# One product moved behind the next step's cosines, and two table products moved from GpSimd to VectorE, in the second block of a two-block float32 kernel

## The chip, the cores and the metric

The kernel runs on 1 core of a Trainium2 chip. The metric is the device time of one execution in microseconds; for a comparison, the median of several executions. Before the change three executions took 1615.61, 1616.44 and 1616.86 us, so the median is 1616.44 us.

Five engines work on instruction queues of their own and wait for one another through semaphores: TensorE (PE; its weight loads are the row PEld), VectorE (DVE), ScalarE (ACT), GpSimd (POOL) and SyncE (SP), which here issues most of the DMAs. Each engine takes its own instructions in order: an instruction that waits holds up all that stand behind it on that engine.

## The reference, cut to what matters

The program has two blocks. The first (an attention with a conditioning state, then a soft mixture of 64 experts) ends before anything the change touches. The second block works on 2 sequences of 1024 tokens with 256 features and runs two layers of this form, of which the change touches two places, the tables of the rotary embedding and the layer norm ahead of the feed-forward part:

```python
def _layer(x, wqkv, qs, ksc, wo, lg, lb, w1, b1, w2, b2):
    h = shift_token(x)
    q, k, v = jnp.split(h @ wqkv, 3, axis=-1)     # 8 heads of 64
    q = l2norm(q) * qs
    k = l2norm(k) * ksc
    q, k = rotary_xpos(q, k)                      # q*cos*scale + rotate_half(q)*sin*scale; k the same with 1/scale
    o = local_attention(q, k, v)                  # windows of 128 tokens, each with the one before it
    x = x + o @ wo
    h = shift_token(x)
    mu, var = h.mean(-1, keepdims=True), h.var(-1, keepdims=True)
    h = (h - mu) / jnp.sqrt(var + 1e-05) * lg + lb
    a, g = jnp.split(h @ w1 + b1, 2, axis=-1)
    x = x + (a * jax.nn.gelu(g, approximate=False)) @ w2 + b2
```

All is float32.

## The kernel before, in words

**Windows and chunks.** The second block cuts the work of its two layers into 32 windows of 128 tokens for the attention (16 for a layer: 2 sequences of 8) and 8 chunks of 512 tokens for the norm and the feed-forward part (4 for a layer). One Python loop, `for s in range(-2, LAG + 4 * CHUNKS)` with `LAG = 7`, staggers them. In step s the loop projects window s + 2 (`project`, L1121, then `rotate_parts`), computes the scores of window s (`scores`, L1210, and `maxima`, L1227), turns the weights of window s - 1 (`turn_e`, L1271 on PE) and mixes window s - 2 with its values (L1290). At the end of the step `forward(s - LAG)` does a quarter of a chunk: for quarters 0 to 2 two slices of `gate` each (L1371), in quarter 2 also `centre` of the next chunk, in quarter 3 `normalise` of the next chunk and `feed`. For the first chunk no chunk runs ahead of it, so `forward(-2)` in step 5 is `centre(0)` alone, `forward(-1)` in step 6 is `normalise(0)` alone, and `forward(0)` in step 7 begins with `gate(0, 0)`.

**The order.** In this loop the order of PE, VectorE, ScalarE and GpSimd is written out by hand (`manual_schedule` over these four): each runs its instructions in the order of the Python calls. Only the DMA queue of SP is ordered by the framework's planner.

**What `rotate_parts(i)` issues, in order:** ScalarE copies the projected queries and keys `pq` from PSUM to `raw` (L1135) and squares them (L1137). VectorE multiplies `pq` by the cosine tables into `t1` (L1143, "the cosines" below; it starts after L1135). GpSimd multiplies the two swapped halves of `raw` by the sine tables into `t2` (L1145, two instructions, "the sines").

**PSUM buffers.** `two_banks` hands out three buffers in turn. In a step after the sixth they go to `pq`, to the two halves of the scores `sc`, then to `pe` (weights of the window before, first half of the heads), `pt` (L1195) and `pe` again (second half), and then to the gates. So the first `pe` writes where `pq` stood and must wait for L1135 and L1143 to have read it; `pt` writes where the first half of `sc` stood, and the second `pe` where the second half stood, and these wait for the maxima (L1227) on VectorE.

**`normalise(f)`** sums the squares on PE (`pvar`, L1333), makes the inverse root on ScalarE as Ln and Exp (L1353, L1354, each with a table load before it), multiplies `hc` by it on VectorE (L1355, 128x1024) and then scales and shifts `hc` on GpSimd (L1357, two instructions of 128x512). `gate` reads `hc`.

**`divide(i, hg)`** divides the weights of window i by their sums: a reciprocal on VectorE (L1256), then four products of 128x256 (L1260), for the first half of the heads on GpSimd and for the second half on VectorE. It stands at the end of a step: the first half ahead of `forward`, the second behind it.

**`weights2(l, ...)`** loads a layer's weights. For `"tabs"` it loads two tiles of tables by SP (L1019): tile y = 0 holds the cosine tables of q and k, tile y = 1 the sine tables. Each of a tile's two halves is multiplied by the layer's `q_scale` or `k_scale` row (for the sines: rolled by half), 128x512, so four products in all, all on GpSimd (L1021). For the second layer the call stands at the very end of step 13, behind `divide(13, 1)`. The cosines and sines of window 16, the second layer's first, come at the start of step 14.

Of the kernel before, what the change touches and what calls it, by code (L numbers as in the profile page):

```python
# [82 lines left out]
def bcast(ap, axis, n):  # L83

    ap = ap.unsqueeze(axis)
    shape = list(ap.shape)
    shape[axis] = n
    return ap.to_broadcast(shape)
# [3 lines left out]
def tile_kernel(ctx: ExitStack, tc: tile.TileContext, a: dict, out: bass.AP):  # L92
    nc = tc.nc
# [768 lines left out]
    def fetch(i, jj):  # L862
        at = slice(jj * 512, (jj + 1) * 512)
        nc.sync.dma_start(row(i)[:, at], lgd[i][:, at])
# [13 lines left out]
    def scale(i):  # L878
        den = dens.pop(i)
        nc.vector.reciprocal(den, den)  # L880
        nc.vector.tensor_scalar(row(i), row(i), den, None, ALU.mult)
# [84 lines left out]
    y = [mo1.tile([P, NE // 4, D], F32, name="y0"), xp.tile([P, NE // 4, D], F32, tag="y1", name="y1")]  # L966
    dxs = ExitStack()
    dx = dxs.enter_context(tc.tile_pool(name="dx", bufs=2))
    with tc.manual_schedule(
        engines={mybir.EngineType.PE, mybir.EngineType.DVE, mybir.EngineType.Activation}  # L970
    ):
        at_weigh = (1, 3, 4, 6)
        for g in range(2):
            weights(g)
        for it in range(3, ITS):
            n, m = divmod(it, 8)
            if it + 1 < ITS:
                logits(it + 1)
            dispatch(it)
            if n and m in (1, 4):  # L980
                experts(4 * n - 4 + m // 4 * 2)

            i = it - ITS + 8
            if 0 <= i < 4:
                for jj in range(4):
                    fetch(i, jj)
            if i - 1 in at_weigh:
                scale(at_weigh.index(i - 1))
            if i in at_weigh:
                heaviest(at_weigh.index(i))  # L990
                weigh(at_weigh.index(i))
        turn_w(0, 0)
        turn_w(0, 1)
        experts(12)
        combine(0, 0)
        turn_w(0, 2)
        combine(0, 1)
        turn_w(0, 3)
        combine(0, 2)
        experts(14)  # L1000
        dxs.close()
        for t in (xa, xb):
            nc.gpsimd.memset(t[:, :, :, 0:1], 0.0)


        load = {}
        wqo = pphi.tile([P, 4 * D * 4], F32, tag="phi", name="wqo")
        load["wqkv"] = wqo[:, : 6 * INNER].rearrange("p (k n) -> p k n", k=2)
        load["wo"] = wqo[:, 6 * INNER :].rearrange("p (k n) -> p k n", k=4)
        mask = dx0.tile([P, 4 * WIN], F32, tag="l1", name="mask")  # L1010
        nc.sync.dma_start(mask, a["mask"])

        def weights2(l, *names):
            for name in names:
                if name == "tabs":

                    load[name] = [dx0.tile([P, 2, 8, DH], F32, tag="dsp", name=f"tabs{l}{y}") for y in range(2)]
                    for y, t in enumerate(load[name]):
                        nc.sync.dma_start(t, a["tabs"].rearrange("p (x y) w d -> y p x w d", y=2)[y])  # L1019
                        for x, of in enumerate((("qs", "ks"), ("qsr", "ksr"))[y]):  # L1020
                            nc.gpsimd.tensor_tensor(  # L1021
                                t[:, x], t[:, x], bcast(rows[:, ROWS[f"{of}{l}"]], 1, 8), ALU.mult
                            )
                    continue
                k = {"wqkv": 2, "wo": 4, "w1": 2, "w2": NF}[name]
                whole = HID // P if name == "w2" else k
                nc.sync.dma_start(
                    load[name][:, :whole, :], a[name][l, : whole * P].rearrange("(c p) n -> p c n", p=P)
                )
                if whole < k:  # L1030
                    for r0 in (0, TG):
                        nc.sync.dma_start(load[name][r0 : r0 + TAIL, whole, :], a[name][l, whole * P :])

        weights2(0, "wqkv", "tabs", "wo")
# [38 lines left out]
    with tc.manual_schedule(  # L1073
# [10 lines left out]
        ts, nrqs, vs, es, eTs, pos, oTs, hcs, us = {}, {}, {}, {}, {}, {}, {}, {}, {}  # L1084
# [45 lines left out]
        def rotate_parts(i):  # L1130

            w = i % NWIN
            pq = pqs.pop(i)
            raw = dx0.tile([P, 16, DH], F32, tag="keep", name="raw")
            nc.scalar.copy(raw, pq)  # L1135
            sqs[i] = la.tile([P, 16, DH], F32, tag="t", name="sq", bufs=3)
            nc.scalar.activation(sqs[i], raw, AF.Square)  # L1137
            t1 = la.tile([P, 16, DH], F32, tag="t", name="t1", bufs=3)
            t2 = la.tile([P, 16, DH], F32, tag="t2", name="t2", bufs=1)
            hf = DH // 2  # L1140
            p4, r4, t14, t24 = (t.rearrange("p (x h) d -> p x h d", x=2) for t in (pq, raw, t1, t2))
            cos, sin = (t[:, :, w, :] for t in load["tabs"])
            nc.vector.tensor_tensor(t14, p4, bcast(cos, 2, H1), ALU.mult)  # L1143
            for lo, hi in ((0, hf), (hf, DH)):
                nc.gpsimd.tensor_tensor(  # L1145
                    t24[:, :, :, lo:hi], r4[:, :, :, hf - lo : DH - lo], bcast(sin[:, :, lo:hi], 2, H1), ALU.mult
                )
            ts[i] = t1, t2
# [167 lines left out]
        def chunk(f):  # L1316

            return f // (B * 2), f // 2 % B, f % 2 * 512
# [28 lines left out]
        def normalise(f):  # L1347
            l, b, t0 = chunk(f)
            hc, sq = hcs[f], hcs.pop((f, "sq"))
            pv = bank("pvar")  # L1350
            sums(f, pv, [sq[:, k, :] for k in range(2)])
            rs = fa["rs"]
            nc.scalar.activation(rs, pv, AF.Ln, bias=eps5)  # L1353
            nc.scalar.activation(rs, rs, AF.Exp, scale=-0.5)  # L1354
            nc.vector.tensor_tensor(hc, hc, bcast(rs, 1, 2), ALU.mult)  # L1355
            for k in range(2):
                nc.gpsimd.tensor_scalar(  # L1357
                    hc[:, k, :], hc[:, k, :], col(f"lg{l}", k), col(f"lb{l}", k), ALU.mult, ALU.add
                )
# [29 lines left out]
        def feed(f):  # L1389

            l, b, t0 = chunk(f)
            hcs.pop(f)
            py, u = two_banks("py"), us.pop(f)
            for c in range(2):
                for n in range(NW1):
                    nc.tensor.matmul(  # L1396
                        py[:, c, :], load["w2"][:, n, c * P : (c + 1) * P], u[:, n, :], start=(n == 0), stop=False
                    )
            for c in range(2):
                r = slice(c * TG, c * TG + TAIL)  # L1400
                nc.tensor.matmul(
                    py[:, c, :], load["w2"][r, NW1, c * P : (c + 1) * P], u[r, NW1, :], start=False, stop=True
                )
            at = slice(1 + t0, 1 + t0 + 512)
            for c in range(2):
                if l < DEPTH - 1:
                    nc.vector.scalar_tensor_tensor(
                        xa[:, c, b, at], py[:, c, :], col(f"b2{l}", c), xb[:, c, b, at], ALU.add, ALU.add
                    )
                    continue  # L1410
                yo = fa["yo"][:, c, :]
                nc.sync.dma_start(yo, xkeep[f % 4][:, c, :])
                nc.gpsimd.tensor_tensor(yo, yo, xb[:, c, b, at], ALU.add)
                nc.vector.scalar_tensor_tensor(yo, py[:, c, :], col(f"b2{l}", c), yo, ALU.add, ALU.add)
                nc.sync.dma_start(out[c * P : (c + 1) * P, b * S + t0 : b * S + t0 + 512], yo)

        def forward(at):

            f, k = divmod(at, 4)
            if at == -2:  # L1420
                centre(0)
            if at == -1:
                normalise(0)
            if not 0 <= f < CHUNKS:
                return
            if k == 0:
                gate(f, 0)
                gate(f, 1)
            if k == 1:
                gate(f, 2)  # L1430
                gate(f, 3)
            if k == 2:
                gate(f, 4)
                if f + 1 < CHUNKS:
                    centre(f + 1)
                gate(f, 5)
            if k == 3:
                if f + 1 < CHUNKS:
                    normalise(f + 1)
                feed(f)  # L1440


# [29 lines left out]
        LAG = 7  # L1472
        fa = {}
        for s in range(-2, LAG + 4 * CHUNKS):
            now, before, nxt, new = (0 <= s + d < WINDOWS for d in (0, -1, 1, 2))

            if new:
                project(s + 2)
                rotate_parts(s + 2)
            ended = 0 <= s - 2 < WINDOWS  # L1480


# [56 lines left out]
            if s == 5:  # L1539

                f = xp.tile([P, 4 * NS], F32, tag="e", name="f")
# [141 lines left out]
```

## Time and profile before

One execution was profiled. It took 1615.51 us by itself, 0.93 us less than the median of the three; the span from its first to its last instruction is 1613.6 us.

| what | number | where from |
|---|---|---|
| median of the three executions | 1616.44 us | the times |
| the profiled execution's own time | 1615.51 us | the times |
| its span | 1613.6 us | the page |
| mean granted TensorE clock | 0.999 | the clock of the core |
| idle time of PE ahead of L1271, ended by L1143 | 4.0 us in 2 waits, the longest 2.5 | the waits of PE |
| the product with the inverse root, L1355 | 8 times, 1.226 us median | the groups by line |
| idle time of VectorE ahead of L1355 | 28.3 us in 8 waits | the groups by line |
| table products on GpSimd, L1021 | 8 times, 1.274 us median | the groups by line |
| the table DMAs of the second layer, L1019 | issued from 1158.7 us, landed within 5.4 us | the rows on the tables |

A row of a timeline gives the start in us from the span's start, the duration in us, the engine, the line of the kernel, the operation, the tile that is written and those that are read, the shape and the count of instructions that were merged into the row. At the end, in square brackets, stands how long the engine had idled and what released it.

### The profile page before, as it was taken

What the parts mean: (1) busy time and instruction counts of PE and PEld (TensorE: products, weight loads), DVE (VectorE), ACT (ScalarE), POOL (GpSimd) and SP (SyncE); (2) the same over time, 40 slices, a digit from 0 to 9 for tenths busy, and PEclk for the clock granted to TensorE, in tenths of its full rate; (3) what the DMA queues carried; (4) which work ended last, traced back from release to release, by engine and by line L of the source; (5) the groups of instructions that cost most, each with busy time, mean ns of one, the idle gap of its engine ahead of it and who ended that gap; (6) DMA issues with size and microseconds to landing.
All of it is one profiled execution on the core that took longest, in us unless ns stands there. A gap on an engine that the chain in (4) does not pass through costs nothing.

```text
span 1613.6 us, 22646 instructions
## 1 busy us (share of the span) xinstructions
PE 1583.7 (98%) x8660; PEld 803.9 (50%) x8660; DVE 910.0 (56%) x1597; ACT 892.6 (55%) x1662; POOL 539.4 (33%) x830
## 2 busy tenths in 40 slices
PE   8999999999999999999999999999999999999998
PEld 4333333333333444444887666555555555656543
DVE  5768758776773222225355765656575665656532
ACT  2477768777886222226134454666656565666631
POOL 4223323333330100000103345545465555555411
PEclk9999999999999999999999999999999999999999
DMA  5100000010000544555632102000100001000001
GB/s 158 53 14 14 1 15 13 1 21 8 1 1 26 170 137 143 165 168 174 205 124 78 40 1 81 1 1 1 66 1 1 14 1 55 1 8 21 14 13 39
DMA packets 49708, 82.66 MB, mean 51 GB/s; under 512 B 4536, under 2 KB 24928, under 8 KB 49344
## 3 DMA queue, kind: packets, MB, share of 16 engines
q1 hardware_dynamic: 47056, 75.38, 15.2%
q0 software_dynamic: 1584, 5.29, 1.1%
q8 instruction: 68, 1.11, 0.3%
q10 hardware_dynamic: 960, 0.56, 0.1%
q14 instruction: 40, 0.33, 0.1%
HBM read 56.04 MB, written 20.97 MB: 48 GB/s over the span
## 4 chain that ended last, share of the span: by engine, by line
PE 92%; DVE 4%; ACT 1%; issue 1%; DMA 1%; POOL 0%; DVEq 0%; ACTq 0%; POOLq 0%
PE pga L1371 9%; PE sc L329 8%; PE po L347 7%; PE pm L295 7%; PE lg L795 7%; PE sl L821 7%; PE pq L1121 6%; PE cmb L909 5%; PE py L1396 4%; PE pwo L1310 3%; PE sc L1210 3%; PE pe L1271 3%; PE po L1290 3%; PE pv L1177 3%; PE pqk L265 2%; PE py L842 2%
## 5 line engine op out<-in xcount | busy, mean ns | idle before, releaser
L302 DVE TENSOR_REDUCE mx<-pm 128x2 f32<-128x1024 f32 x256 | 302.3, 1219 | 118.2 <-PE pm L295 117.6
L337 ACT ACTIVATE e<-sc 128x512 f32<-128x512 f32 (+1 forms) x500 | 266.1, 611 | 72.2 <-PE pm L295 44.6
L329 PE MATMUL sc<-qs,km 32*128 32x512 f32 x1024 | 254.7, 619 | 0.9 <-DVE qs L317 0.9
L295 PE MATMUL pm<-km,qm 32*128 32x512 f32 x1024 | 246.1, 619 | 2.4 <-ACT xa L432 0.6
L365 POOL TENSOR_TENSOR ob<-ob,part 128x512 f32<-128x512 f32 x101 | 128.3, 1271 | 270.2 <-ACT part L364 270.2
L1260 POOL TENSOR_SCALAR e<-e,den 128x256 f32<-128x256 f32 (+1 forms) x128 | 130.9, 1036 | 31.3 <-DVE den L1256 31.3
L1371 PE MATMUL pga<-hc,w 128*128 128x512 f32 x320 | 141.1, 593 | 0.0
L347 PE MATMUL po<-e,v 128*32 128x512 f32 x1024 | 136.7, 604 | 0.0
L1145 POOL TENSOR_TENSOR t<-raw,tabs 128x512 f32<-128x512 f32 x64 | 81.7, 1299 | 154.7 <-ACT raw L1135 149.4
L329 PEld LDWEIGHTS sc<-qs,km 32*128 32x128 f32 x1024 | 87.6, 183 | 84.6 <-ACT e L337 64.4
L1244 ACT ACTIVATE e<-e,nmx 128x256 f32<-128x256 f32 (+1 forms) x256 | 123.6, 487 | 2.7 <-DVE nmx L1227 2.5
L1121 PE MATMUL pq<-wqo,xa 128*128 128x512 f32 x256 | 115.9, 595 | 1.6 <-DVE xb L897 0.9
L909 PE MATMUL cmb<-xb,y 128*128 128x256 f32 x512 | 116.6, 380 | 0.2 <-ACT xb L895 0.2
L795 PE MATMUL lg<-phi,xa 128*128 128x512 f32 x256 | 115.9, 595 | 0.3 <-ACT xa L432 0.3
L821 PE MATMUL sl<-dsp,xb 128*128 128x512 f32 x256 | 114.9, 592 | 0.0
L295 PEld LDWEIGHTS pm<-km,qm 32*128 32x128 f32 x1024 | 82.9, 183 | 60.0 <-DVE mx L302 31.6
L1227 DVE CUSTOM_DVE_ANT_0 e<-sc,mask,zn 128x256 f32<-128x256 f32 (+1 forms) x256 | 101.9, 460 | 17.3 <-PE sc L1210 17.3
L909 PEld LDWEIGHTS cmb<-xb,y 128*128 128x128 f32 x512 | 94.9, 190 | 16.6 <-issue 3.2
L805 DVE TENSOR_TENSOR l<-lg,keep 128x512 f32<-128x512 f32 x32 | 22.1, 691 | 143.5 <-ACT keep L803 143.5
L1371 PEld LDWEIGHTS pga<-hc,w 128*128 128x128 f32 x320 | 59.2, 190 | 67.2 <-issue 65.1
L1135 ACT COPY raw<-pq 128x1024 f32<-128x1024 f32 x32 | 32.4, 1012 | 107.2 <-PE pq L1121 105.4
L803 ACT COPY keep<-lg 128x512 f32<-128x512 f32 x32 | 18.7, 585 | 125.1 <-issue 107.4
(213 smaller groups left out, 2456.2 us busy)
## 6 DMA issues: line engine op xcount, KB each, us to landing
lgd<-keep SPq DMA_DIRECT2D x64, 256.0 KB, 2.4
w<-in_ffn_W SPq DMA_DIRECT2D x16, 1024.0 KB, 7.0
ebig<-lgd SPq DMA_DIRECT2D x64, 256.0 KB, 3.3
wqo<-in_wqkv SPq DMA_DIRECT2D x2, 1536.0 KB, 7.5
w<-in_w SPq DMA_DIRECT2D x2, 1386.0 KB, 5.9
km<-hk SPq DMA_DIRECT2D x32, 64.0 KB, 2.3
qm<-hq SPq DMA_DIRECT2D x32, 64.0 KB, 2.4
phi<-in_phi SPq DMA_DIRECT2D x1, 2048.0 KB, 7.6
```

Source lines behind the costliest of these rows:

```text
L295: nc.tensor.matmul(pm[:, x, :], qm[u % 2][r, i * P : (i + 1) * P], km[u % 3][r, n * 512 : (n + 1) * 512], start=True, stop=True,)
L302: nc.vector.tensor_reduce(mxs[hu][:, i % 4, 2 * half : 2 * half + 2, n], pm, AX.X, ALU.max)
L329: nc.tensor.matmul(sc[:, x, :] if both else sc[x], km[u % 3][r, j * P : (j + 1) * P], qs[u % 2][r, n * 512 : (n + 1) * 512], start=True, s ...
L337: nc.scalar.activation(part, t, AF.Exp, scale=1.0 / HD0**0.5)
L347: nc.tensor.matmul(po[32 * hh : 32 * hh + 32, :], v[b][:, j, at : at + 32], es[s, hh // 2][:, hh % 2, :], start=True, stop=True,)
L365: nc.gpsimd.tensor_tensor(obs[u, n], obs[u, n], part, ALU.add)
L795: nc.tensor.matmul(lg[:, b, :], xa[:, k, b, 1 + m * P : 1 + (m + 1) * P], phi[:, k, n * 512 : (n + 1) * 512], start=(k == 0), stop=(k == 1),)
L821: nc.tensor.matmul(accs[n][b][:, c, :], xo_tm[:, b * 8 + m, c * P : (c + 1) * P], d[:, b, :], start=(m == 0), stop=(m == 7),)
L909: nc.tensor.matmul(acs[q][:, c, :], y[b][:, 4 * jj + j, c * P : (c + 1) * P], eT[:, j // 2, j % 2 * 256 : (j % 2 + 1) * 256], start=(jj == ...
L1121: nc.tensor.matmul(pq[:, x, :], shifted(xa, k, b, w * WIN, P), load["wqkv"][:, k, x * 512 : (x + 1) * 512], start=(k == 0), stop=(k == 1),)
L1260: engine.tensor_scalar(e[:, x, c, lo:], e[:, x, c, lo:], den[:, x, c : c + 1], None, ALU.mult)
L1371: nc.tensor.matmul(pt[:, x, :], load["w1"][:, k, lo : lo + P], hcs[f][:, k, :], start=(k == 0), stop=(k == 1))
```

## The change

Two edits. First, `normalise` is cut in two: the sums and the inverse root stay, and the products (VectorE's L1355 and GpSimd's two of L1357) go into a new function `normalised`. For every chunk but the first it is called right behind `normalise`, which leaves the order as it was. For the first chunk it is called in step 7, behind `project(9)` and `rotate_parts(9)`: on VectorE the product then stands behind the cosines of window 9 and ahead of the maxima of window 7, on GpSimd the two instructions stand behind the sines of window 9. Second, of the second layer's four table products the two of the cosine tables (y = 0) are issued on VectorE, at the same place in the program. The first layer's four stay on GpSimd. No DMA is added, removed or moved.

```diff
@@ weights2, "tabs" @@
                         for x, of in enumerate((("qs", "ks"), ("qsr", "ksr"))[y]):
-                            nc.gpsimd.tensor_tensor(
+                            (nc.gpsimd if y or l == 0 else nc.vector).tensor_tensor(
                                 t[:, x], t[:, x], bcast(rows[:, ROWS[f"{of}{l}"]], 1, 8), ALU.mult
                             )
@@ normalise @@
             rs = fa["rs"]
             nc.scalar.activation(rs, pv, AF.Ln, bias=eps5)
             nc.scalar.activation(rs, rs, AF.Exp, scale=-0.5)
+            hcs[f, "rs"] = rs
+
+        def normalised(f):
+            l = chunk(f)[0]
+            hc, rs = hcs[f], hcs.pop((f, "rs"))
             nc.vector.tensor_tensor(hc, hc, bcast(rs, 1, 2), ALU.mult)
             for k in range(2):
                 nc.gpsimd.tensor_scalar(
@@ forward @@
             if k == 3:
                 if f + 1 < CHUNKS:
                     normalise(f + 1)
+                    normalised(f + 1)
                 feed(f)
@@ the loop over s @@
             if new:
                 project(s + 2)
                 rotate_parts(s + 2)
+            if s == LAG:
+                normalised(0)
             ended = 0 <= s - 2 < WINDOWS
```

## The prediction

> **What bounds the kernel now.** I read the page's busy shares first, then the waits of PE, then the timeline around each wait.
>
> ```profile
> PE 1583.7 (98%) x8660; PEld 803.9 (50%) x8660; DVE 910.0 (56%) x1597; ACT 892.6 (55%) x1662; POOL 539.4 (33%) x830
> ```
>
> PE is busy for 98% of the span and every other engine for 56% or less. So only time in which PE stands still can be won, and any work that makes PE stand still costs. In the waits of PE (line, releaser, us in total, times, longest) from 850 us on, the second block, one row leads; the next has 0.9 us.
>
> ```profile
> PE pe L1271 <- DVE t L1143: 4.0, 2, 2.5
> ```
>
> Twice in the program the first `pe` of a step waits for VectorE's cosines, which free its buffer. The timelines show the two: they are step 7 and step 14, the two places that the change touches. So 4.0 us, 0.25%, is the most that it can win. Step 7:
>
> ```profile
> 1031.82 0.69 DVE L1171 TENSOR_TENSOR t<-t,zn 128x512 f32<-128x512 f32 x1 [1.00 <-POOL zn L1164]
> ...
> 1034.58 0.63 ACT L1354 ACTIVATE f<-f 128x512 f32<-128x512 f32 x1
> 1035.12 0.99 ACT L1135 COPY raw<-pq 128x1024 f32<-128x1024 f32 x1
> 1035.24 1.30 DVE L1355 TENSOR_TENSOR hc<-hc,f 128x1024 f32<-128x1024 f32 x1 [2.73 <-ACT f L1354]
> ...
> 1036.67 1.88 DVE L1260 TENSOR_SCALAR e<-e,den 128x256 f32<-128x256 f32 x4
> ...
> 1038.38 2.51 POOL L1145 TENSOR_TENSOR t<-raw,tabs 128x512 f32<-128x512 f32 x2
> 1038.47 1.20 DVE L1143 TENSOR_TENSOR t<-pq,tabs 128x1024 f32<-128x1024 f32 x1
> ...
> 1039.83 1.06 PE L1271 MATMUL pe<-ident,e 128*128 128x128 f32 x8 [2.49 <-DVE t L1143]
> ```
>
> VectorE stands still for 2.73 us until the inverse root (L1354) comes. Behind L1355 wait the four divisions L1260 (step 6's second half), and behind those the cosines, though `raw` is done at 1036.11. PE idles for 2.49 us. Step 14:
>
> ```profile
> 1179.08 4.68 DVE L1260 TENSOR_SCALAR e<-e,den 128x256 f32<-128x256 f32 x4
> ...
> 1179.66 1.01 ACT L1135 COPY raw<-pq 128x1024 f32<-128x1024 f32 x1 [1.48 <-PE pq L1121]
> ...
> 1179.77 5.12 POOL L1021 TENSOR_TENSOR tabs<-tabs,rows 128x512 f32<-128x512 f32 x4
> ...
> 1183.68 1.21 DVE L1143 TENSOR_TENSOR t<-pq,tabs 128x1024 f32<-128x1024 f32 x1
> ...
> 1184.95 1.09 PE L1271 MATMUL pe<-ident,e 128*128 128x128 f32 x8 [1.50 <-DVE t L1143]
> 1184.97 2.51 POOL L1145 TENSOR_TENSOR t<-raw,tabs 128x512 f32<-128x512 f32 x2
> ```
>
> What the cosines wait for here is not the tables: their two products on POOL are over by 1182.3 (two of 1.28 us from 1179.77). It is VectorE's own divisions, which take 4.68 us for the four, where most steps have 1.14 (0.35 each). Narrow windows show why: the second runs from 1179.76 to 1181.19, the third ends at 1182.48, the fourth at 1183.76, each some 0.15 us behind the end of one of POOL's table products. So a VectorE product from SBUF gets through only where a POOL TENSOR_TENSOR ends. A second row shows the same for a VectorE TENSOR_TENSOR with both inputs in SBUF:
>
> ```profile
> 1087.65 1.09 POOL L1326 TENSOR_TENSOR f<-xb 128x512 f32<-128x512 f32 x1 [4.48 <-DVE xb L1314]
> ...
> 1088.17 1.65 DVE L1170 TENSOR_TENSOR t<-t,t 128x1024 f32<-128x1024 f32 x1
> ...
> 1088.71 1.89 POOL L1260 TENSOR_SCALAR e<-e,den 128x256 f32<-128x256 f32 x1
> ```
>
> L1170 takes 1.19 us when free. Here it takes 1.65 and ends 1.08 us behind L1326's end (1088.74); POOL's next, usually 0.92, is held until then. So at a boundary the waiting VectorE instruction goes first, and then POOL waits. The cosines read PSUM and one SBUF tile, and stay at 1.20 to 1.23 beside the sines.
>
> **Part one, step 7.** ScalarE's order is untouched, so `raw` still ends at 1036.11. VectorE goes from L1171 (ends 1032.51) to the reciprocal (0.16) and the four divisions. These run beside POOL's own divisions; in step 6 the same meeting took 1.73 us. They end near 1034.4, with 1.7 us to spare. The cosines follow `raw`: 1036.14 to 1037.36 (step 6: 0.03 behind `raw`, 1.22 long). PE followed them by 0.15 in this step, so it starts `pe` at 1037.51: 2.32 us earlier.
>
> What is late next is the second `pe`. The product L1355 now stands between the cosines and the maxima. It reads two SBUF tiles, and it is queued at 1037.28 while the first sine product runs (from about 1036.18, 1.27 long, to 1037.45). By the L1326 row it goes at that boundary and ends some 1.1 us later, at 1038.57 (unhindered: 1037.28 + 1.23 = 1038.51). The second sine product waits for it. The eight maxima took 3.31 us from first start to last end in this step (1039.60 to 1042.91); they now run from 1038.49 to 1041.80. The second `pe` needs the buffer that the last four read. PE would be there 3.49 us behind the first `pe` (1039.83 to 1043.32), at 1041.00, and starts at about 1041.95. Before it was 1043.32. So of 2.32 us, 0.95 is given back: **part one wins 1.4 us**. POOL: the sines end by 1039.8, L1357 (two of 0.88 beside VectorE) by 1041.6; the gates need it at 1042.8, so that cover is 1.2 us. The bounds: 2.5 won (the whole stall, if nothing is late next), and nothing won.
>
> **Part two, step 14.** No wait on a DMA is new in effect: VectorE's table products need the tables, which landed by 1164.8 (issued by 1159.4, at most 5.4 us). Queued behind them on VectorE are the cosines and the maxima. POOL is left with two table products, but the sines stand right behind them and `raw` is ready at 1180.67. So POOL still issues four TENSOR_TENSORs in a row, 1179.77 to 1184.89, two of them now L1145 (1.27 against 1.28). VectorE's divisions are held as before and end at 1183.76. The first table product is queued at 1183.68, when POOL's fourth has run since 1183.57, and waits for it until 1184.89.
>
> A VectorE table product is not in the trace. The nearest row is L1171, the same 128x512 from two SBUF tiles, 0.69 us; the far one is POOL's 1.28 for the same work. I take 0.69, since L1171 is the same engine and shape. The first ends 0.58 behind the boundary (0.11 less than alone, as L1170 did), at 1185.47; the second at 1186.08 (queued 0.08 before the first ends); the cosines at 1187.21 (1.21 less 0.08). PE followed by 0.06 here: 1187.27 against 1184.95. **Part two costs 2.3 us.** Everything behind it moves by the same: the maxima still end 3.2 us behind the first `pe`, and the second comes 3.5 behind it. Bounds: 1.5 won, if POOL doesn't hold VectorE at all (divisions 1.14 from 1179.08, two products 1.38, cosines 1.21: over by 1182.8, and PE comes at 1183.45); 3.5 lost, if POOL goes first at every boundary.
>
> **Two rules of the Trainium skill.** SBUF — State Buffer, section Who interferes with whom, says that VectorE's product with a scalar per partition can hold, and be held by, a GpSimd instruction for its whole length. Step 6's row differs: beside POOL's TENSOR_SCALAR, VectorE's divisions take 0.53 each, not POOL's 0.92. By the rule step 7's divisions would end at about 1036.07 in place of 1034.4, still ahead of `raw`: the sum would stay. Perfetto Trace Analysis, section Optimizing Scalar/DVE Operations, warns that moving work between these two engines might not help, as they share a read port. It speaks against part two, and the rows above give it a price; a reading by durations alone (0.69 on VectorE in place of 1.28 on POOL) would call it a gain of some 0.6 us for each product.
>
> **The sum:** 2.3 - 1.4 = +0.9 us. On the profiled execution's own 1615.51 (span 1613.6 and 1.9 around it) that is 1616.4; that execution was 0.9 below the median, so for the median I say 1616.44 + 0.9 = **1617.3 us**. A difference under 0.2% (3.2 us) is about what a measurement of this kernel can't tell from no change.
>
> **Rivals.**
> - *As it is meant (faster).* If POOL's two remaining table products and the sines don't hold VectorE, step 14's stall goes whole: -1.5, with part one -2.9 us, 1613.5. If L1355 is not late for the second `pe` either, -4.0, 1612.4. For it: POOL has only half the table work. Against: the sines are ready to follow, and are TENSOR_TENSORs too. 13%, of which 4% beyond 0.2%.
> - *Table products before the last sine.* If the first slips in at 1183.7, both end at 1184.9, the cosines at 1186.1: part two costs 1.3, and the sum is -0.1, 1616.3. Against: POOL's fourth was issued 0.1 us earlier. 9%.
> - *The second sine before L1355.* Then L1355 ends 1.3 us later, the maxima at 1043.1, the second `pe` at 1043.2: part one wins 0.1 and the sum is +2.2, 1618.6. The margin is about 0.17 us. 13%.
> - *POOL first at every boundary (slower).* The divisions of step 14 wait until 1184.89, end at 1185.7, the table products at 1187.1, the cosines at 1188.3, PE 3.5 late; and step 7 wins nothing: +3.5 us, 1619.9. It decides if a waiting VectorE instruction doesn't go first. Against: the L1170 row, and the divisions of step 14. 7%.
> - The forecast: 58%, its own range +0.2 to +1.7.
>
> The range from 1615.2 to 1619.4 leaves out the first rival and most of the last. Beyond 0.2%: faster 4%, slower 8%, the rest within.
>
> **What the profile after would show.** Step 7: L1355 behind L1143, the first `pe` without a wait or with one under 0.3, the second with one of some 0.9 on L1227, one L1145 of over 2 us. Step 14: L1260 still near 4.7 us for four, the first L1021 on DVE about 1.7 long, the second about 0.7, and PE idle for 3.8 us on L1143 in place of 1.50. I am wrong if L1260 falls towards 1.14, or if the second `pe` of step 7 doesn't move.

## The result, and the profile after

The changed kernel takes 1618.97 us (median of 19 executions, 1617.85 to 1620.11) against 1616.23 us before (19 executions, 1615.46 to 1617.10). The ratio is 1.0017, 95% interval 1.0011 to 1.0023: slower by 2.7 us. That lies in the stated range and within 0.2%, but it is three times the +0.9 us of the sum.

The profiled execution is the longest of the 19: 1620.11 us by itself, span 1618.1. PE's waits from 850 us on still begin with the same row (line, releaser, us in total, times, longest):

```profile
PE pe L1271 <- DVE t L1143: 4.3, 2, 4.1
...
PE pe L1271 <- DVE nmx L1227: 0.5, 1, 0.5
```

The total has hardly moved, 4.3 for 4.0. But it was 2.5 and 1.5, and now it is 0.2 and 4.1: the stall of step 7 is gone, that of step 14 has grown, and a third one, on the maxima, is new. The timeline of step 7 (L1355 and L1357 of before are L1360 and L1362 here):

```profile
1033.19 1.68 DVE L1260 TENSOR_SCALAR e<-e,den 128x256 f32<-128x256 f32 x4
...
1036.69 1.23 DVE L1143 TENSOR_TENSOR t<-pq,tabs 128x1024 f32<-128x1024 f32 x1 [1.83 <-ACT raw L1135]
1036.75 3.50 POOL L1145 TENSOR_TENSOR t<-raw,tabs 128x512 f32<-128x512 f32 x2 [0.20 <-ACT raw L1135]
1037.84 1.28 DVE L1360 TENSOR_TENSOR hc<-hc,f 128x1024 f32<-128x1024 f32 x1
...
1038.07 1.07 PE L1271 MATMUL pe<-ident,e 128*128 128x128 f32 x8 [0.18 <-DVE t L1143]
...
1040.24 1.51 POOL L1362 TENSOR_SCALAR hc<-hc,cols 128x512 f32<-128x512 f32 x2
```

VectorE's wait is now one for `raw`, and the product stands behind the cosines. The two sines take 3.50 us in place of 2.51: the second was held until the product had ended. This execution had lost 0.55 us to the other before it came here (0.33 of it in its first 25 us; PE's mixing product ahead of `pe` starts at 1035.92 against 1035.37). Set against that, the first `pe` starts 2.31 us earlier.

Step 14:

```profile
1178.22 4.75 DVE L1260 TENSOR_SCALAR e<-e,den 128x256 f32<-128x256 f32 x4
...
1178.92 2.56 POOL L1021 TENSOR_TENSOR tabs<-tabs,rows 128x512 f32<-128x512 f32 x2
...
1181.56 2.53 POOL L1145 TENSOR_TENSOR t<-raw,tabs 128x512 f32<-128x512 f32 x2
...
1182.90 2.34 DVE L1021 TENSOR_TENSOR tabs<-tabs,rows 128x512 f32<-128x512 f32 x2
1185.34 1.23 DVE L1143 TENSOR_TENSOR t<-pq,tabs 128x1024 f32<-128x1024 f32 x1
1186.71 1.94 PE L1271 MATMUL pe<-ident,e 128*128 128x128 f32 x8 [4.11 <-DVE t L1143]
1188.45 3.62 PE L1177 MATMUL pv<-wqo,xa 128*128 128x512 f32 x4
...
1193.03 1.04 PE L1271 MATMUL pe<-ident,e 128*128 128x128 f32 x8
```

Two rows of before at this place, `pv` and the second `pe`, to hold beside them:

```profile
1185.88 1.88 PE L1177 MATMUL pv<-wqo,xa 128*128 128x512 f32 x4
...
1188.47 1.04 PE L1271 MATMUL pe<-ident,e 128*128 128x128 f32 x8
```

GpSimd still runs four TENSOR_TENSORs in a row, the divisions still take 4.75 us, and the first table product on VectorE takes 1.74 and the second 0.68. PE idles for 4.11 us. The rows of the first `pe` and of `pv` show what the prediction had not counted: the transposes `pe` take 1.94 us for eight (1.09 before), and `pv` 3.62 for four (1.88 before). The same work, on the same engine, takes nearly twice as long. The busy times by stretch have the granted clock in their third column from the end (the columns: stretch, us, then busy us of PE, PEld, DVE, ACT and POOL, the clock, the DMA share, GB/s):

```profile
1178.00:1183.00 5.00, 4.60 (x50) 3.19 (x48) 4.96 (x7) 2.42 (x3) 4.60 (x5) 1.00 0.00 0
1183.00:1187.00 4.00, 0.29 (x2) 0.32 (x3) 3.90 (x6) 0.23 (x1) 1.09 (x1) 0.83 0.00 0
1187.00:1189.00 2.00, 2.00 (x9) 1.78 (x8) 2.00 (x11) 0.31 (x1) 0.00 (x0) 0.50 0.04 8
1189.00:1191.00 2.00, 2.00 (x3) 0.67 (x2) 1.97 (x6) 1.98 (x2) 0.00 (x0) 0.50 0.00 0
1191.00:1193.00 2.00, 2.00 (x10) 1.37 (x9) 0.31 (x2) 1.99 (x10) 1.16 (x6) 0.64 0.00 0
1193.00:1195.00 2.00, 2.00 (x13) 1.47 (x12) 0.90 (x1) 2.00 (x6) 1.42 (x7) 1.00 0.01 4
```

The granted clock falls to 0.50 towards the end of the stall, 1.09 us before PE resumes, and is back at 1.00 after 6.83 us (1185.62 to 1192.45 in the trace), 5.74 us after PE has resumed. Before, it was 1.00 in all the stretches of this place.

Where the time went can be read by following one and the same PE instruction in both traces. Ahead of step 7 the changed kernel is 0.55 us late. At the second `pe` of step 7 it is 0.91 early (1042.41 against 1043.32): part one won 1.46. At the first `pe` of step 14 it is 1.76 late (1186.71 against 1184.95): the stall cost 2.67. At the second `pe` of the same step it is 4.56 late (1193.03 against 1188.47): the clock cost 2.80 more, and from there nothing changes. For the median, 1616.23 - 1.46 + 2.67 gives 1617.4 without a clock term, and 1618.97 leaves 1.5 for the clock. That 1.5 is a net figure: some executions of the kernel before pay for a drop of their own in step 7, which part one takes away (see the experiments). The executions spread over 2.3 us (before: 1.6), which suggests that the drop does not cost the same each time.

**The theories.** H: part one wins; part two costs what the held VectorE instructions cost, and PE's long stall lowers its clock besides. Rivals: the loss comes from part one (P); VectorE's added work, 0.69 us a product, is the cost of part two (W); the stall is all and the clock has no part in it (N).

### The profile page after: what moved, and what is told of

The parts are those of the page before. It is cut to its first block, busy times and chain, and to the rows that moved or that the text cites. A ratio compares the mean times of both kernels' runs of the same rounds, so it can differ in the third digit from the quotient of the medians.

```text
span 1618.1 us, 22648 instructions
## 1 busy us (share of the span) xinstructions
PE 1587.4 (98%) x8660; PEld 805.5 (50%) x8660; DVE 912.3 (56%) x1599; ACT 892.4 (55%) x1662; POOL 536.6 (33%) x828
## 4 chain that ended last, share of the span: by engine, by line
PE 91%; DVE 5%; ACT 2%; issue 1%; DMA 1%; POOL 0%; DVEq 0%; ACTq 0%; POOLq 0%
PE pga L1376 9%; PE sc L329 8%; PE po L347 7%; PE pm L295 7%; PE lg L795 7%; PE sl L821 7%; PE pq L1121 6%; PE cmb L909 5%; PE py L1401 4%; PE pwo L1310 3%; PE po L1290 3%; PE pe L1271 3%; PE sc L1210 3%; PE pv L1177 3%; PE pqk L265 2%; PE py L842 2%
```

## Experiments

Each is compared with the kernel before, timed beside it on the same chip. The median of "before" was 1616.81 us beside the first four, 1616.23 beside the second four and 1616.32 beside the last three.

**Each part alone.** The first kernel is the change with all table products on GpSimd:

```diff
-                            (nc.gpsimd if y or l == 0 else nc.vector).tensor_tensor(
+                            nc.gpsimd.tensor_tensor(
```

> Part one alone: the first chunk's product stands behind the cosines of window 9, all four table products of the second layer stay on GpSimd. Theory H (a VectorE instruction from SBUF is held by a running GpSimd TENSOR_TENSOR, and the long stall of PE that follows in step 14 also lowers the granted clock; part one wins): the first pe of step 7 starts 2.3 us earlier, the second 1.4 us, step 14 is as before with PE idle for 1.5 us at a granted clock of 1.00; 1614.8 us against 1616.2 before. Rival P (the loss comes from part one): 1616.2 or more.

Measured: 1614.54 us, ratio 0.9985 (0.9977 to 0.9994), 2.3 us less than before. In its trace the first `pe` of step 7 waits 0.2 us, the second 0.5, step 14 waits 1.5 as before. Part one is a gain; P falls. The gain is larger than the 1.46 of the stalls; see below for the clock in step 7.

The second is the kernel before with the table line of the change alone:

```diff
-                            nc.gpsimd.tensor_tensor(
+                            (nc.gpsimd if y or l == 0 else nc.vector).tensor_tensor(
```

> Part two alone: the product stays where it was, the two cosine tables of the second layer are multiplied on VectorE. Theory H: PE idles for 4.1 us in step 14 (2.6 more than before), and then runs at half the granted clock for some us, which costs 0.4 to 2.7 more; 1619.2 to 1621.5 us, near 1620.4. Rival W (VectorE's added work is the whole cost: two products of 0.69 us, no clock): 1617.6 us. Rival P: 1616.2 or less.

Measured: 1620.94 us, ratio 1.0027 (1.0017 to 1.0037), 4.1 us more. PE idles for 4.11 us in step 14 and the clock is at 0.50 behind it. The cost is well above W's 1.4. In this execution the clock also fell in step 7, behind the stall of 2.49 us that the kernel before has too:

```profile
1040.21 1.22 PE L1271 MATMUL pe<-ident,e 128*128 128x128 f32 x8 [2.49 <-DVE t L1143]
1041.21 3.47 PE L1177 MATMUL pv<-wqo,xa 128*128 128x512 f32 x4
```

There `pv` takes 3.47 us where the first trace of the kernel before has 1.88, and PE loses 1.7 us by `pt`.

**More work on VectorE.** All four table products of the second layer go to VectorE, two more than in the change:

```diff
-                            (nc.gpsimd if y or l == 0 else nc.vector).tensor_tensor(
+                            (nc.gpsimd if l == 0 else nc.vector).tensor_tensor(
```

> The change with all four table products of the second layer on VectorE, two more than the change has. Theory H: GpSimd has nothing to run while VectorE divides, since its sines wait for the tables; the four divisions take about 1.8 us in place of 4.7, the four products 2.5, the cosines end some 0.3 us earlier than before, PE idles for about 1.2 us and the granted clock stays at 1.00; 1614.6 us. Rival W (each product on VectorE adds its 0.69): 1.4 more than the changed kernel, 1620.4 us.

Measured: 1614.15 us, ratio 0.9984 (0.9975 to 0.9993), 2.7 us less than before, where W expects a time above the changed kernel's. The timeline of step 14:

```profile
1178.02 1.55 DVE L1260 TENSOR_SCALAR e<-e,den 128x256 f32<-128x256 f32 x4
...
1179.49 2.48 DVE L1021 TENSOR_TENSOR tabs<-tabs,rows 128x512 f32<-128x512 f32 x4
...
1181.90 1.21 DVE L1143 TENSOR_TENSOR t<-pq,tabs 128x1024 f32<-128x1024 f32 x1
1182.21 2.51 POOL L1145 TENSOR_TENSOR t<-raw,tabs 128x512 f32<-128x512 f32 x2 [3.57 <-DVE tabs L1021]
...
1183.26 1.07 PE L1271 MATMUL pe<-ident,e 128*128 128x128 f32 x8 [0.86 <-DVE t L1143]
```

GpSimd now idles until the tables are there, so it holds nothing: the divisions take 1.55 us, four table products 2.48 (the change: 2.34 for two), and PE waits 0.86 us. Twice the work on VectorE makes the stall 3.25 us shorter. What cost the change its time was not VectorE's work but what GpSimd ran beside it. The stall that H expected was 1.2.

**The clock.** The changed kernel, with work for PE in the stall of step 14:

```diff
             beside(s, "a")
+            if s == 14:
+                warm = bank("warm")
+                for k in range(4):
+                    nc.tensor.matmul(warm, ident, mask, start=(k == 0), stop=(k == 3))
             if before:
                 turn_e(s - 1, 0)
```

> The changed kernel with four matrix products of 128x512 more (3.4 us of PE), whose result nothing reads, queued on PE in step 14 ahead of the first pe, where PE idles for 4.1 us. Theory H: they fill the stall, the granted clock stays at 1.00 behind it, the pv products take 0.43 us each in place of 0.85; 1617.4 us, 1.5 less than the changed kernel although PE does more. Rival N (the stall alone is the cost, the clock has nothing to do with it): 1619.0 as the changed kernel, or up to 3.4 more where the added products aren't hidden.

Measured: 1616.98 us, ratio 1.0003 (0.9994 to 1.0011). The changed kernel's interval, 1.0011 to 1.0023, lies above that ratio, and the two intervals only touch. PE has a row of 3.70 us of work more (L1511) and the program is faster: 0.2 us above its kernel before, where the changed kernel is 2.7 above. The stretches behind the filled stall, the clock third from the end:

```profile
1187.00:1189.00 2.00, 2.00 (x11) 1.36 (x11) 2.00 (x11) 1.01 (x1) 0.00 (x0) 1.00 0.04 8
1189.00:1191.00 2.00, 2.00 (x16) 1.64 (x15) 2.00 (x7) 1.98 (x4) 0.00 (x0) 1.00 0.00 0
```

The first `pe` starts as late as in the changed kernel (1.93 later than before, from 0.75 early at the end of step 7: 2.68), so the held VectorE instructions cost the same. Only the clock differs, and N falls. By the distances of the two medians from the kernel before, 2.7 and 0.2 us, the drop costs 2.6 us; by the ratios it costs 2.3.

**One table product on VectorE:**

```diff
-                            (nc.gpsimd if y or l == 0 else nc.vector).tensor_tensor(
+                            (nc.gpsimd if y or x or l == 0 else nc.vector).tensor_tensor(
```

> The change with one table product of the second layer on VectorE, one less than the change has. Theory H: GpSimd still runs five TENSOR_TENSORs in a row; the divisions are held as before, the product waits for the fourth, the cosines follow it 0.6 us later; PE idles for about 3.4 us in step 14 (4.1 in the changed kernel). By the stalls 0.5 us more than before; with the clock's drop behind a stall of 3.4 us up to 2.7 more than that. Rival W (each product on VectorE adds 0.69 and no more): 0.7 us less than the changed kernel, with or without the clock.

Measured: 1616.83 us, ratio 1.0002 (0.9993 to 1.0011). The stall is 2.33 us, not 3.4. I had the order at one boundary wrong:

```profile
1178.58 3.84 POOL L1021 TENSOR_TENSOR tabs<-tabs,rows 128x512 f32<-128x512 f32 x3
...
1182.49 0.68 DVE L1021 TENSOR_TENSOR tabs<-tabs,rows 128x512 f32<-128x512 f32 x1
1182.50 3.02 POOL L1145 TENSOR_TENSOR t<-raw,tabs 128x512 f32<-128x512 f32 x2
1183.30 1.23 DVE L1143 TENSOR_TENSOR t<-pq,tabs 128x1024 f32<-128x1024 f32 x1
1184.58 1.85 PE L1271 MATMUL pe<-ident,e 128*128 128x128 f32 x8 [2.33 <-DVE t L1143]
```

GpSimd's third table product ends at 1182.42; the sines start 0.08 later, and the VectorE product was queued 0.01 ahead of them. It goes first, unhindered (0.68), and this time the sines wait (3.02 for two). By the medians the kernel is 2.1 us faster than the changed one, where W has 0.7. In the changed kernel GpSimd's last sine was queued 0.12 us before VectorE's product (1182.78 and 1182.90). In these two traces a tenth of a microsecond decides who waits for whom. Even behind 2.33 us the clock fell to 0.50 here, and `pe` took 1.85.

**Both edits in other places.** The product between the divisions and the cosines, with all table products on GpSimd:

```diff
-            if s == LAG:
-                normalised(0)
...
             if now:
                 divide(s, 1)
+            if s == LAG - 1:
+                normalised(0)
```

> Part one in another place: the first chunk's product stands behind step 6's divisions and ahead of the cosines of window 9 (not behind them); the four table products stay on GpSimd. In step 7 VectorE stands idle between the divisions (over by about 1.7 us ahead of raw) and raw; the inverse root comes 0.9 us ahead of raw's end, so the product of 1.3 us goes there and delays the cosines by 0.35 us only, and the maxima no longer have it ahead of them. Theory H: first pe 2.0 us earlier than before, the second 2.0 too (1.4 in the first place), PE idle for 0.5 us there; 2.0 us less than before by the stalls, up to 0.9 less again by the clock. Rival (the second pe was late for another reason than the product ahead of the maxima): the second pe gains 1.4 at most.

Measured: 1613.77 us, ratio 0.9984 (0.9975 to 0.9992), 2.5 us less than before. The first `pe` waits for 0.57 us and the second for nothing. From the start of the step to the second `pe` PE wins about 1.9 us, against 1.46 in the change's place: the maxima were indeed late for the product ahead of them. The times alone can't tell the two places apart (0.9984 here, 0.9985 for the product alone in the change's place).

The table products behind the norms of step 13, all still on GpSimd, and nothing else:

```diff
             if new:
                 norms(s + 2)
+            if s + 2 == B * NWIN - 1:
+                weights2(1, "tabs")
...
             if s + 2 == B * NWIN - 1:
-                weights2(1, "wqkv", "tabs")
+                weights2(1, "wqkv")
```

> The kernel before with one edit: the second layer's four table products, all on GpSimd, stand behind the norms of step 13, where GpSimd is idle for some 5 us and VectorE waits for the attention's output product, instead of at the step's end. Theory H: no GpSimd TENSOR_TENSOR runs beside the divisions at the end of step 13; the four take about 1.6 us, the cosines follow raw at once, PE's idle time of 1.5 us in step 14 goes; 1.5 us less than before. Rival (the cosines waited for the tables or for something else): the time of before.

Measured: 1615.39 us, ratio 0.9990 (0.9981 to 0.9999), 0.8 us less, half of the 1.5 expected, in an interval that reaches to 3.1. The stall of step 14 is gone:

```profile
1166.91 4.96 POOL L1021 TENSOR_TENSOR tabs<-tabs,rows 128x512 f32<-128x512 f32 x4
...
1180.31 1.55 DVE L1260 TENSOR_SCALAR e<-e,den 128x256 f32<-128x256 f32 x4
1180.89 1.01 ACT L1135 COPY raw<-pq 128x1024 f32<-128x1024 f32 x1 [1.48 <-PE pq L1121]
1181.99 1.22 DVE L1143 TENSOR_TENSOR t<-pq,tabs 128x1024 f32<-128x1024 f32 x1
...
1184.61 1.09 PE L1271 MATMUL pe<-ident,e 128*128 128x128 f32 x8
```

This execution is 1.23 us late when it comes here (`raw` starts at 1180.89 against 1179.66); it lost that ahead of step 7, so not by the edit. The first `pe` is 0.34 early, so step 14 won 1.57 us, as H has it.

Both together, with the tables' work split as in the change (cosines on VectorE, sines on GpSimd):

> Both edits in other places: the product ahead of the cosines, behind the divisions, and the table products behind the norms of step 13, the two of the cosines on VectorE and the two of the sines on GpSimd. Theory H: both stalls go but for 0.5 us, 3.5 us less than before by the stalls, up to 0.9 less again by the clock; faster than the kernel before and the changed one. Rival: the gains don't add, 2.0 less at most.

Measured: 1612.25 us (1611.87 to 1612.79), ratio 0.9972 (0.9961 to 0.9983), 4.0 us less than before. Of all the kernels here this is the fastest. It has the changed kernel's split of the work; only the places differ. PE has one wait of 0.6 us left on the cosines, in step 7.

**The clock behind a stall of 2.5 us.** The kernel before with two of the products of the filled stall, in step 7 (`if s == LAG`, `range(2)`):

> The kernel before with two matrix products of 128x512 more (1.7 us of PE), whose result nothing reads, queued on PE in step 7 ahead of the first pe, where PE idles for 2.49 us. The times of the kernel before lie in two groups, about 1615.3 to 1616.4 and 1616.8 to 1617.7. Theory H (behind a stall of 2.5 us the granted clock drops in some executions and not in others): with the stall cut to 0.8 us the upper group goes, the median is about 1615.9, 0.3 to 0.6 less than before, and no time is above 1616.6. Rival N (the groups have another cause): two groups as before, the median unchanged, or more where the added products aren't hidden.

Measured: 1616.32 us against 1616.32, ratio 0.9999 (0.9990 to 1.0008). The median didn't move, against the expectation. The upper group is gone: none of 11 times is above 1616.44, where 5 of the 15 of the kernel before, timed beside it, are 1616.80 to 1617.01. That agrees with H but doesn't settle it. Two further traces of the kernel before should have caught a drop:

> The kernel before as it is, one look, for the clock behind its stall of 2.49 us in step 7. Theory H: either the pv products behind it take 0.43 us each, or two or three of them 0.85, and then the span is over 1 us longer than the 1613.6 of the first look. Rival N: always 0.43.

> The kernel before as it is, a further look; the same is expected as of the look before it. With two looks beside the two that show a stall of 2.49 us so far without a drop (the kernel before, the early tables) and the one with a drop (the tables alone), theory H expects at least one of the two to show it.

Neither did: both have the stall of 2.50 us and the clock at 1.00 behind it, in spans of 1613.7 and 1614.2. So of the six traces with a stall of 2.3 to 2.5 us (the kernel before three times, the early tables, the tables alone, one product on VectorE) two show a drop; of the two with 4.11 us both do; no stall of 1.5 us or less in these two steps does.

Why the drop comes once and not the next time can be read from the clock's record in the traces. The drops of steps 7 and 14 last 3.413 us (twice) or 6.827 us (twice, behind 4.11 us). In each of the 13 traces every change of the clock lies a whole number of steps of 3.413 us behind the first one; in the tables alone, for instance, the drop of step 14 begins 146.77 us, 43 such steps, behind that of step 7. The clock thus changes only on a grid. Laid over the stalls, it gives PE's idle time (a window's length less PE's busy time in it) in the two windows of the grid that a stall touches, and the clock that follows each:

| trace, step | idle in the first window, us | idle in the second, us | clock behind the first | clock behind the second |
|---|---|---|---|---|
| before, first trace, 7 | 0.60 | 1.89 | 1.00 | 1.00 |
| before, second, 7 | 0.85 | 1.64 | 1.00 | 1.00 |
| before, third, 7 | 1.47 | 1.03 | 1.00 | 1.00 |
| early tables, 7 | 0.84 | 1.64 | 1.00 | 1.00 |
| tables alone, 7 | 2.48 | 0.00 | 0.50 | 1.00 |
| one product on VectorE, 14 | 2.32 | 0.00 | 0.50 | 1.00 |
| tables alone, 14 | 2.23 | 1.87 | 0.50 | 0.50 |
| the change, 14 | 3.02 | 1.08 | 0.50 | 0.50 |
| the change, stall filled, 14 | 0.00 | 0.49 | 1.00 | 1.00 |

A window with 2.23 us of idle time or more is followed by 0.50, one with 1.89 or less, if it ran at 1.00, by 1.00. A stall of 2.5 us lowers the clock when it lies within one window and not when two windows share it evenly enough, and where the grid lies differs from execution to execution. The limit holds for these stalls alone: at the program's end 1.58 us were enough in the filled stall's trace. How much of the 2.3 us that the product alone won is the clock stays open; beyond the 1.46 of the stalls it is 0.8.

## Why the prediction was right and where it was wrong

- **What bounds the kernel, and the two stalls:** right. The two traces part in steps 7 and 14, beside 0.55 us that were lost ahead of both. That 4.0 us is the most to be won was not: it counts the stalls alone, and the kernel with both edits in other places won 4.0 with 0.6 us of stall left.
- **Part one, 1.4 us:** right. Measured 1.46: the first `pe` 2.31 earlier (2.32 in the sum), the second held by the maxima for 0.53 us as idle time and some more in `pt`. The product went ahead of the second sine, so that rival did not occur.
- **Part two's stall, 2.3 us:** the mechanism was right: the divisions as slow as before, the first table product held until GpSimd's fourth had ended. The size was off by 0.35 (measured 2.67, with PE idle for 4.11 in place of 3.8). Half of that is the cosines: they start 0.10 us behind the second table product, on which they wait, where the sum let them start 0.08 ahead of its end.
- **The step that failed** is this sentence of part two: "Everything behind it moves by the same". It priced a stall by its length alone. Behind 4.1 us the granted clock was at 0.50 for 6.83 us, 5.74 of them with PE at work, which cost 2.80 us in the profiled execution and, against the filled stall, 2.3 to 2.6 in the median. The sum had no term for it, and no rival had one. The row was not to be had from the stalls in the second block of the first trace, since none of them showed a drop; but the Trainium skill has the rule, and it went unused. TensorE: Matmul & The Clock Gate, section Part 1, says that TensorE falls to half its clock after an idle window of about 3.4 us and is back after as much sustained work, with windows that run freely. The traces agree with the figure (steps of 3.413 us) and with windows that run freely, but a window didn't have to be idle throughout: 2.23 to 3.02 us of idle time in it were enough. So 4.11 us did it in both traces, and 2.33 and 2.49 us in two of six.
- **"Beyond 0.2%: faster 4%, slower 8%, the rest within":** the ratio 1.0017 lies within 0.2%, though its interval reaches beyond. That the time lies in the stated range is in part luck: +2.7 us is above the forecast's own +0.2 to +1.7, and the room up there was kept for the rivals with +2.2 and +3.5, neither of which occurred.
- **The price of the moved products by durations alone** (0.69 in place of 1.28, a gain of some 0.6 us each), which the prediction set aside, is refuted: two products on VectorE made the stall of step 14 2.6 us longer in place of 1.2 shorter, and one made it 0.8 longer.

## What to carry to other kernels

Moving an instruction from GpSimd to VectorE shortens nothing if GpSimd fills the gap with its next instruction of the same kind and VectorE is held by that; look at which pairs run side by side, not at the engines' sums, and put such products where the other engine is idle. A product that the critical wait doesn't need belongs into a wait that is there anyway: one place earlier, ahead of the cosines, PE won 1.9 us by it, one place later 1.46. And when a stall of the matrix engine is forecast, price its length and also the clock behind it: at about 4 us it was paid in both traces, at about 2.4 in two of six, by where the stall lay between the clock's steps.

## What the runs showed of the hardware that was not expected

- Four products of 128x512 on VectorE with GpSimd idle (2.48 us) took hardly longer than two beside GpSimd's TENSOR_TENSORs (2.34 us).
- The order of two instructions queued within 0.01 to 0.12 us of each other on the two engines decided who was held. With one product on VectorE the stall was 2.33 us, where the order of the changed kernel would have given about 3.4 by an estimate from its rows.
- Idle TensorE time of 4.11 us, all but 0.49 of it filled with products that nothing reads, made the program 2.3 to 2.6 us faster.
- Stalls of one length, 2.5 us, lowered the clock or didn't: the clock changed only on a grid of 3.413 us, and fell when 2.23 us or more of idle time lay in one of its windows.
